# A decoder layer with a mixture of experts: the routing of two batches stepped beside the experts' items, its count products and statistics pinned in trace order

## The chip, the core and the metric

The kernel runs on one core of one Trainium2 chip. The core has five engines, each with a queue of its own: TensorE (PE in the profile; its weight loads are PEld), VectorE (DVE), ScalarE (ACT), GpSimd (POOL), and SyncE (SP), which here only starts transfers. An engine runs its queue in order; semaphores let one engine wait for another. The metric is the time of one execution on the device in microseconds (us), as the median of several runs. A profile comes from one execution, which has a time and a span of its own.

## What is computed

Four batches of 512 tokens of 256 elements pass through three layers. Each is added to its input and normalised. The first is a selective state space layer, the second a gated attention over a context, the third a mixture of eight experts of which each token takes two:

```python
x = _layernorm(x + _L0_attn_ref(x, ...))
x = _layernorm(x + _L0_xattn_ref(x, ctx_1024, ctx_1024, ...))
x = _layernorm(x + _L0_ffn_ref(x, gate_w, w1, w2, w3))

def _L0_ffn_ref(hidden_states, gate_w, w1, w2, w3):
    ...
    logits = x @ gate_w
    mult, sel = _sparse_mixer_routing(logits)      # the two best experts and their weights
    w = jnp.sum(mult[:, :, None] * (sel[:, :, None] == jnp.arange(E)[None, None, :]), axis=1)
    h = jax.nn.silu(jnp.einsum('th,ehf->etf', x, w1)) * jnp.einsum('th,ehf->etf', x, w3)
    out = jnp.einsum('etf,efh,te->th', h, w2, w)
```

The change touches the end of the second layer and the beginning of the third.

## The kernel before

**Who sets the order.** The kernel is written on a library that plans it: the code is traced once, and a planner then fills each engine's queue. By its own estimates of durations it takes, whenever an engine is free, the instruction whose inputs are ready, and of several the one traced first. So the trace order is a priority, not the order on the chip, and the queues are fixed before the kernel runs. `tc.keep_in_program_order(ins)` forbids the planner one thing: to put `ins` ahead of the instruction traced just before it on the same engine. It adds no wait on the chip. Only what is later in the trace can still overtake a pinned instruction, if that one isn't ready.

**Attention** (`attend_fast`). Work goes by pairs (batch b, pair of heads p), eight in all. The loop over n = 0 to 8 (L1178) has four turns each, `tb`. A turn traces the scores of pair n (`pq`, L1026, then `ct` on ScalarE, L1037, and the triangle on GpSimd, L1038), the values of pair n-1 (`ph`, L1046), and in the first turn the gather of pair n-2 (`gather`, L1051): `ph` is copied to `hT`, turned by products into `pth` (L1060), and `hraw` (L1064) takes it from there. PSUM for `pth` comes from a pool of two banks, `pt`, which later also holds the experts' transposes.

**The tail of a batch.** After the second pair of a batch is gathered, `finish(b)` (L1084) becomes a generator in the list `tails`. `step()` (L1166) runs one piece of the first tail; the loop calls it twice per turn (L1199, L1200). Counting pieces from 0, they are, before:

- 0: scales `den`, `vr` (with a square root on ScalarE). 1: the logits `base` (L1110 to L1120), then the first choice (`route`, L1683). 2: the second choice. 3: `hv` (L1127) on VectorE and the sum with x1 on GpSimd (L1134).
- 4 (`close`, L1800): `hot` (L1713), the mark of the chosen experts, then `norm_stats` (L59): four times `bn_stats` (L64) and `bn_aggr` (L65) on VectorE, a square root on ScalarE (L67), a reciprocal.
- 5: the count products, five of them (L1717), and `rstd`. 6: the normalised rows `x` on ScalarE (L1815) and their writes to `xds` and `yd` by SP (L1820).
- 7: positions of tokens, from `posm` (L1727) to `hi` (L1739). 8: `olo` (L1745), eight times `oval` (L1750) and a position product (L1754). 9 and 10: `by` (L1765) and the tables of tokens, weights and destinations (`tables`, L1644). 11: the weights of the two experts (L1776 to L1789, with Exp). 12: a transpose of them (L1792), and their writes to `wds` by SP (L1798).

Batch b's tail is appended in turn 0 of n = 2b + 3, so batch 2's pieces 0 to 7 are traced at n = 7 and 8 to 12 at n = 8; batch 3's tail is appended after the loop and is traced as a whole between two calls of `work` (L1934).

**The experts.** `work` (L1339) takes items in a line. An item fetches its token rows with an indirect transfer on GpSimd (`fetch`, L1244; two items ahead), transposes them (L1277, copied to `xgT`, L1281), and runs `up` (L1284): chunks of 16 (one block of 128 tokens) or 8 products (two blocks) into `pu` (L1292), Silu on ScalarE (L1297), `ht` on VectorE (L1298), with a yield after each chunk. `pu` has three banks. (The trace shows two instructions for each f32 product; products are counted here as it shows them.) Then `down` of the item before runs (L1316), scaled (L1336) by weights fetched in `weigh` (L1306), and is added to `yd` (L1322).

The **early** items (experts 0 and 1, one block each, four chunks each) need only the tables of batches 0 and 1. The **middle** items (experts 3 to 7, two blocks, eight chunks) need the tables and rows of batch 2, the **late** ones those of batch 3. All of the rest of the kernel is TensorE's work on these items.

Of the kernel before, what the change touches and what calls it, by code (L numbers as in the profile page):

```python
# [2 lines left out]

# [40 lines left out]
def decoder_kernel(ctx: ExitStack, tc: tile.TileContext, t: dict, out: bass.AP):  # L44
    nc = tc.nc
# [10 lines left out]
        nc.sync.dma_start(out=c, in_=src)  # L56
        return c

    def norm_stats(sp, src, n, tag):  # L59

        st = sp.tile([P, n, 6], F32, tag=tag + "st", name=tag + "st")
        mv = sp.tile([P, n, 2], F32, tag=tag + "mv", name=tag + "mv")
        for i in range(n):
            nc.vector.bn_stats(out=st[:, i, :], in_=src[:, i, :])  # L64
            nc.vector.bn_aggr(out=mv[:, i, :], in_=st[:, i, :])  # L65
        sd = sp.tile([P, n], F32, tag=tag + "sd", name=tag + "sd")
        nc.scalar.activation(sd, mv[:, :, 1], AF.Sqrt, bias=eps5)  # L67
# [934 lines left out]
    def attend_fast(ap, hrp, np_, pt, tri, onw, mix, part, gatew, close, rt, route):  # L1002
# [4 lines left out]
        with ExitStack() as hs:  # L1007
# [170 lines left out]
            for n in range(len(pairs) + 1):  # L1178
                nxt = []
                if n and pairs[n - 1][1] == 0:  # L1180
                    hraw = hrp.tile([P, NB, NH, DH + 1 + NE], F32, tag="hraw", name="hraw")
                    sq2 = hrp.tile([P, NB, NH], F32, tag="sq2", name="sq2")
                if n:
                    po = ph.tile([P, S], F32, tag="ph", name="ph")
                for tb in range(NB):
                    if n == B:
                        for _ in late:
                            pass
                    elif n:
                        next(late, None)  # L1190
                    if n < len(pairs) and tb < NB - 1:
                        nxt += scores(*pairs[n], (tb,) if tb < NB - 2 else (tb, tb + 1))
                    if tb == 0 and sums is not None:
                        gathered(*sums)
                    if tb == 1 and n in (1, 1 + NH):
                        residual(n // NH)
                    if n:
                        values(*pairs[n - 1], tb, cts[tb], po)
                    step()  # L1199
                    step()  # L1200
                if n:
                    sums = (*pairs[n - 1], po, hraw, sq2)
                cts = nxt
# [11 lines left out]
    def experts(o, fast):  # L1215
# [120 lines left out]
                nc.scalar.activation(y[:, g, :], ps[:, g, :], AF.Copy, scale=wg[:, g : g + 1])  # L1336
                scatter(yd, v, c, y[:, g, :], compute_op=ALU.add)

        def work(visits, weights, ahead=(), between=None, pending=None):  # L1339

            after = [e for e, _ in (*visits, *ahead)][len(weights) :]
            line = [(n, v, cols) for n, (_, its) in enumerate(visits) for v, cols in its]
            xgs = [fetch(v, cols) for _, v, cols in line[:2]]
            for i, (n, v, cols) in enumerate(line):
                G = len(cols)
                xT_ = turn(xgs.pop(0), G)
                w1, w3, w2 = weights[n]
                ht = inner(G)  # L1350
                for _ in up(xT_, G, w1, w3, ht):
                    pass
                if i + 2 < len(line):
                    xgs.append(fetch(*line[i + 2][1:]))
                if pending is not None:
                    down(*pending)
                pending = (v, cols, ht, w2)
                if (i == 0 or line[i - 1][0] != n) and after and len(weights) < n + 3:
                    weights.append(weights_of(after.pop(0)))
                if between is not None:  # L1360
                    between(i)
            return weights[len(visits) :], pending
# [189 lines left out]
    def layers23(fast):  # L1552
# [4 lines left out]
        with ExitStack() as rest:  # L1557
# [125 lines left out]
            def route(b, base):  # L1683
# [30 lines left out]
                yield  # L1714
                pc = bank[:, 32 : 32 + 5 * NE].rearrange("p (n e) -> p n e", e=NE)
                for i in range(5):
                    nc.tensor.matmul(  # L1717
                        pc, one_b if i else tri_b, hot[:, 4 - i : 9 - i, :],
                        start=(i == 0), stop=(i == 4),
                    )  # L1720
                yield
                NK = 2 * NB
# [26 lines left out]
                for j in range(NK):  # L1749
# [1 line left out]
                        oval[:, j, :], i128, hi[:, j : j + 1],  # L1751
                        vv[:, b * NK + j : b * NK + j + 1], ALU.is_equal, ALU.mult,
                    )
                    nc.tensor.matmul(  # L1754
                        pk, olo[:, j, :], oval[:, j, :], start=(j == 0), stop=(j == NK - 1)
                    )
                nc.vector.tensor_tensor(count, pc[:, NB], count, ALU.add)
                if 1 <= b < B - 1:
# [30 lines left out]
                nc.vector.reciprocal(wk, su)  # L1789
                yield  # L1790

                nc.tensor.transpose(bank[:NK, 384:], wk, ident)  # L1792
                wkT = rt("wkT", [NK, P])
                nc.scalar.copy(wkT, bank[:NK, 384:])
                for v in range(max(b - 1, 0), 3):
# [4 lines left out]
            def close(b, hv, routing=None):  # L1800
# [2 lines left out]
                if routing is None:  # L1803
                    routing = route(b, logits(b, hv))
                next(routing)
                mv, rs = norm_stats(np_, hv, NB, "n2")
                yield
                next(routing)
                rstd[b] = rt("rstd", [P, NB])
                nc.vector.tensor_copy(rstd[b], rs)  # L1810
                ms = np_.tile([P, NB], F32, tag="n2ms", name="n2ms")
# [111 lines left out]
            o.htp, o.sip, o.yp, o.xtp, o.np3, o.fin, o.pup, o.pop, o.x1 = (  # L1923
                htp, sip, yp, xtp, np3, fin, pup, pop, x1
            )
            if tails:
                *done, last = tails
                for tail in done:
                    for _ in tail:
                        pass  # L1930
            else:
                last = iter(())
            weights, pending = xp.work(xp.early, weights, xp.mid)
            for _ in last:  # L1934
                pass
            weights, pending = xp.work(
                xp.mid + xp.late, weights, [xp.final], lambda i: overflow() if i == 1 else None,
                pending,
            )
            return xp.finale(xp.final, weights[0], pending)  # L1940

# [118 lines left out]
```

## Time and profile before

| | |
|---|---|
| median of 3 runs | 681.87 us (680.82 to 684.33) |
| the profiled execution | 681.57 us |
| its span, first to last instruction | 679.7 us |
| granted TensorE clock, mean of the span | 0.978 |
| TensorE busy | 645.8 us (95%) |
| stage from 200 to 292 us: TensorE busy, granted clock | 77.68 of 92 us, 0.89 |
| in the same stage: VectorE, ScalarE, GpSimd busy | 75.02, 52.95, 52.66 us |
| from 292 to 640 us: TensorE busy, granted clock | 348.00 of 348 us, 1.00 |

The granted clock is the share of full speed that the chip's throttle allowed TensorE. A line of the timeline gives the start, the duration, the engine, the line of the kernel and the operation, what it writes and reads, how many are merged, and in brackets the engine's idle time before it and what ended that. A line of the waits names who waited for whom, the total, how often, and the longest. A busy engine isn't one at full speed, and an engine that is idle costs nothing where it isn't the bound.

Four points of the timeline are used below: attention's last values end at 253.78 us, expert 0's first product starts at 262.86, its transposed token rows at 261.68, and the first middle item's first product at 290.50. A batch's GpSimd sums (L1134) take 0.73 us each, four to a batch.

### The profile page before, as it was taken

To read this page: it belongs to the slowest core of one execution; us is meant where nothing else is said; L and a number is where in the kernel's file an instruction comes from. 1 tells how busy PE (TensorE), PEld (TensorE's weight loads), DVE (VectorE), ACT (ScalarE), POOL (GpSimd) and SP (SyncE) were. 2 spreads that over 40 slices of the span, in tenths; PEclk is the share of its full clock that TensorE was granted. 3 is DMA by queue.
4 is the path that set the end of the run, shared out by engine and by line. 5 is a ranking of instruction groups with operands and counts; after the bars stand their busy time and mean duration, and the time that the engine had idled before them with its cause. 6 is when DMAs were issued, how large, how long until landed. Compare 5 with 4: busy or idle time off the path is not lost. (4 is left out here: it accounts for less than half of the span.)

```text
span 679.7 us, 9237 instructions
## 1 busy us (share of the span) xinstructions
PE 645.8 (95%) x3447; PEld 497.9 (73%) x3447; DVE 307.8 (45%) x799; ACT 241.1 (35%) x473; POOL 209.0 (31%) x244
## 2 busy tenths in 40 slices
PE   6999999999997987899999999999999999999994
PEld 2434577766353447788888888888888899999993
DVE  1969658797557899662222221111211121121641
ACT  3965472132775754541121221112111111111452
POOL 0033400000564572743423244322432323423202
PEclk9999999999997996999999999999999999999998
DMA  8300501004603066856755335644463524883531
GB/s 279 121 1 0 186 1 32 31 1 160 242 1 124 9 196 216 285 170 209 220 169 179 86 94 154 194 153 137 150 209 78 152 78 148 272 316 86 176 113 36
DMA packets 61671, 92.89 MB, mean 137 GB/s; under 512 B 8904, under 2 KB 48784, under 8 KB 61360
## 3 DMA queue, kind: packets, MB, share of 16 engines
q1 hardware_dynamic: 52432, 80.51, 34.7%
q0 software_dynamic: 8096, 9.60, 7.2%
q10 hardware_dynamic: 1088, 2.10, 0.9%
q8 instruction: 29, 0.48, 0.3%
q14 instruction: 26, 0.21, 0.1%
HBM read 78.78 MB, written 14.06 MB: 137 GB/s over the span
## 5 line engine op out<-in xcount | busy, mean ns | idle before, releaser
L1292 PE MATMUL pu<-xgT,w 128*128 128x128 f32 (+1 forms) x1600 | 266.3, 327 | 1.0 <-DVE ht L1298 0.9
L1292 PEld LDWEIGHTS pu<-xgT,w 128*128 128x128 f32 x1600 | 243.0, 193 | 22.7 <-ACT x L1391 1.1
L1298 DVE TENSOR_TENSOR ht<-pu,si 128x256 f32<-128x256 f32 x148 | 62.6, 424 | 229.5 <-ACT si L1297 229.2
L1316 PE MATMUL po<-w,ht 128*128 128x256 f32 x592 | 136.7, 381 | 0.0
L1297 ACT ACTIVATE si<-pu 128x256 f32<-128x256 f32 x148 | 56.8, 384 | 195.6 <-PE pu L1292 195.3
L1316 PEld LDWEIGHTS po<-w,ht 128*128 128x128 f32 x592 | 109.8, 191 | 14.6 <-ACT y L1336 0.6
L1322 POOL DMA_INDIRECT yd<-y,tab x33 | 53.3, 1614 | 143.3 <-ACT y L1336 125.7
L232 PE MATMUL xz<-xT,win 128*128 128x512 f32 x128 | 58.3, 616 | 6.3 <-DMA xT<-in_xT 5.8
L1248 POOL DMA_INDIRECT xg<-xd,tab x37 | 36.8, 993 | 82.7 <-PE pt L1277 59.5
L232 PEld LDWEIGHTS xz<-xT,win 128*128 128x128 f32 x128 | 24.9, 198 | 38.8 <-issue 30.4
L1336 ACT ACTIVATE y<-po,wg 128x256 f32<-128x256 f32 x33 | 15.6, 474 | 93.8 <-PE po L1316 93.8
L1038 POOL TENSOR_TENSOR ct<-ct,tri 128x128 f32<-128x128 f32 x64 | 32.7, 530 | 34.0 <-ACT ct L1037 33.4
L460 PE MATMUL fpy<-mt,xs 128*128 128x384 f32 (+3 forms) x128 | 36.8, 438 | 0.5 <-DVE fsz L464 0.5
L255 DVE SCALAR_TENSOR_TENSOR acc<-xp,convw,acc 128x1024 f32<-128x1024 f32 x24 | 29.3, 1286 | 14.2 <-ACT acc L250 14.2
L1037 ACT ACTIVATE ct<-pq,eT 128x512 f32<-128x512 f32 (+3 forms) x64 | 29.9, 524 | 15.3 <-PE pq L1026 15.2
L1307 POOL DMA_INDIRECT wg<-wd,tab x33 | 31.9, 967 | 9.9 <-issue 9.6
L1026 PE MATMUL pq<-x1T,ctxT 64*128 64x512 f32 (+3 forms) x128 | 33.0, 486 | 1.6 <-ACT ct L1037 1.2
L1281 DVE COPY xgT<-pt 128x512 f32<-128x512 f32 (+1 forms) x22 | 12.5, 569 | 41.4 <-PE pt L1277 41.4
L460 PEld LDWEIGHTS fpy<-mt,xs 128*128 128x128 f32 x128 | 22.1, 190 | 12.3 <-issue 6.2
L485 PE MATMUL fpo<-fwout,fsz 128*128 128x256 f32 x128 | 28.9, 382 | 0.1
L485 PEld LDWEIGHTS fpo<-fwout,fsz 128*128 128x128 f32 x128 | 23.8, 190 | 4.7 <-issue 0.8
L1026 PEld LDWEIGHTS pq<-x1T,ctxT 64*128 64x128 f32 x128 | 13.7, 188 | 17.5 <-issue 8.0
(260 smaller groups left out, 612.9 us busy)
## 6 DMA issues: line engine op xcount, KB each, us to landing
w<-in_w SPq DMA_DIRECT2D x57, 1024.0 KB
xd<-x SPq DMA_DIRECT2D x9, 512.0 KB
xT<-in_xT ACTq DMA_DIRECT2D x4, 512.0 KB
ctxT<-in_ctxT SPq DMA_DIRECT2D x1, 2048.0 KB
val<-in_ctx SPq DMA_DIRECT2D x4, 512.0 KB
fxr<-in_x SPq DMA_DIRECT2D x4, 512.0 KB
yd<-x SPq DMA_DIRECT2D x4, 512.0 KB
x<-yd SPq DMA_DIRECT2D x4, 512.0 KB
```

The costliest lines, as they stand in the source:

```text
L232: nc.tensor.matmul(ps, win[:, k, c * P : (c + 1) * P], xT[:, k, b * S : (b + 1) * S], start=(k == 0), stop=(k == 1),)
L460: nc.tensor.matmul(ps[:, j * P :], xs[j][:, c, :], mt[b][j], start=(j == 0), stop=(j == NB - 1),)
L485: nc.tensor.matmul(ps, sz[:, c, b * S + i * P : b * S + (i + 1) * P], wout[:, c, :], start=(c == 0), stop=(c == NC - 1),)
L1026: nc.tensor.matmul(pss[e][:, cols[-1]], ctxT[rows, p, s0 : s0 + P], x1T[rows, p, s0 : (b + 1) * S], start=True, stop=True,)
L1038: nc.gpsimd.tensor_tensor(ct[:, :P], ct[:, :P], tri, ALU.mult)
L1248: nc.gpsimd.indirect_dma_start(out=xg[:, g, :], out_offset=None, in_=xds[min(v, 2)][:, :], in_offset=bass.IndirectOffsetOnAxis(ap=tok[v][: ...
L1292: nc.tensor.matmul(ps[:, j, u, :], w[:, k, (f + u) * P : (f + u + 1) * P], xT_[:, k, :N], start=(k == 0), stop=(k == 1),)
L1297: nc.scalar.activation(si, ps[:, 0].rearrange("p u n -> p (u n)"), AF.Silu)
L1298: nc.vector.tensor_tensor(ht[:, f * N : (f + U) * N], ps[:, 1].rearrange("p u n -> p (u n)"), si, ALU.mult)
L1307: issue = nc.gpsimd.indirect_dma_start(out=wg, out_offset=None, in_=wds[min(v, 2)][:, :], in_offset=bass.IndirectOffsetOnAxis(ap=wat[v][:, ...
L1316: nc.tensor.matmul(ps, ht[:, (f * G + g) * P : (f * G + g + 1) * P], w2[:, f, :], start=(f == 0), stop=(f == NF - 1),)
L1322: return nc.gpsimd.indirect_dma_start(out=rows[:, :], out_offset=bass.IndirectOffsetOnAxis(ap=dest[v][:, c : c + 1], axis=0), in_=src, in_ ...
```

## The change

1. In the loop of `attend_fast`, `step()` isn't called any more at n = 7 and n = 8. The tail of batch 2, which is appended at n = 7, therefore leaves the loop untouched; `tails` then holds the tails of batches 2 and 3.
2. `work` takes an iterator `beside` and advances it once after each chunk of `up`. Before the early items the tail of batch 2 is given to it, and before the middle items that of batch 3, both through `zip_longest` with itself, that is two pieces per chunk. What is left of batch 2's tail after the early items is traced then.
3. In `close`, the piece with `rstd` no longer runs the count products. They come after the normalised rows, as a piece of their own: three pieces behind `hot` in place of one. A tail has 14 pieces now, 0 to 13: the count products are 7, positions 8, position products 9, tables 10 and 11, weights 12, their transpose 13.
4. `bn_stats` of this norm, the count products, the position products and the transpose of the weights are pinned with `keep_in_program_order`.

Piece by chunk, then: batch 2's pieces 0 to 7 follow the four chunks of expert 0, two by two, and 8 to 13 the first three of expert 1; batch 3's follow the first seven of the first middle item's eight chunks. Batches 0 and 1 stay in the loop, with one piece more each.

```diff
-    def norm_stats(sp, src, n, tag):
+    def norm_stats(sp, src, n, tag, keep=False):
...
-            nc.vector.bn_stats(out=st[:, i, :], in_=src[:, i, :])
+            bn = nc.vector.bn_stats(out=st[:, i, :], in_=src[:, i, :])
+            if keep:
+                tc.keep_in_program_order(bn)
             nc.vector.bn_aggr(out=mv[:, i, :], in_=st[:, i, :])
...
-                    step()
-                    step()
+                    if n < len(pairs) - 1:
+                        step()
+                        step()
...
-        def work(visits, weights, ahead=(), between=None, pending=None):
+        def work(visits, weights, ahead=(), between=None, pending=None, beside=iter(())):
...
                 for _ in up(xT_, G, w1, w3, ht):
-                    pass
+                    next(beside, None)
...
                 for i in range(5):
-                    nc.tensor.matmul(
-                        pc, one_b if i else tri_b, hot[:, 4 - i : 9 - i, :],
-                        start=(i == 0), stop=(i == 4),
+                    tc.keep_in_program_order(
+                        nc.tensor.matmul(
+                            pc, one_b if i else tri_b, hot[:, 4 - i : 9 - i, :],
+                            start=(i == 0), stop=(i == 4),
+                        )
                     )
...
-                    nc.tensor.matmul(
-                        pk, olo[:, j, :], oval[:, j, :], start=(j == 0), stop=(j == NK - 1)
+                    tc.keep_in_program_order(
+                        nc.tensor.matmul(
+                            pk, olo[:, j, :], oval[:, j, :], start=(j == 0), stop=(j == NK - 1)
+                        )
                     )
...
-                nc.tensor.transpose(bank[:NK, 384:], wk, ident)
+                tc.keep_in_program_order(nc.tensor.transpose(bank[:NK, 384:], wk, ident))
...
                 next(routing)
-                mv, rs = norm_stats(np_, hv, NB, "n2")
+                mv, rs = norm_stats(np_, hv, NB, "n2", True)
                 yield
-                next(routing)
                 rstd[b] = rt("rstd", [P, NB])
...
-            if tails:
-                *done, last = tails
-                for tail in done:
-                    for _ in tail:
-                        pass
-            else:
-                last = iter(())
-            weights, pending = xp.work(xp.early, weights, xp.mid)
-            for _ in last:
+
+            *done, last = tails or [iter(())]
+            third = chain(*done)
+            third = zip_longest(third, third)
+            weights, pending = xp.work(xp.early, weights, xp.mid, beside=third)
+            for _ in third:
                 pass
             weights, pending = xp.work(
                 xp.mid + xp.late, weights, [xp.final], lambda i: overflow() if i == 1 else None,
-                pending,
+                pending, zip_longest(last, last),
             )
```

More of the change, by code (lines that the diff above doesn't have):

```diff
@@ L1 @@
 from contextlib import ExitStack
+from itertools import chain, zip_longest
 from types import SimpleNamespace
```

## The prediction, made before the changed kernel was run

> **What bounds the kernel now.** I read the busy shares first, then the slices, then the waits of TensorE, then its timeline where the slices show a hole. Columns of the first fence: busy microseconds with the share of the span, and the span in 40 slices of 17 us, in tenths.
>
> ```profile
> PE 645.8 (95%) x3447; PEld 497.9 (73%) x3447; DVE 307.8 (45%) x799; ACT 241.1 (35%) x473; POOL 209.0 (31%) x244
> ...
> PE   6999999999997987899999999999999999999994
> ...
> DVE  1969658797557899662222221111211121121641
> ...
> PEclk9999999999997996999999999999999999999998
> ```
>
> TensorE is the bound: 9 in nearly every slice, and all of the time from 292 to 640 us (the windows view gives 348.00 of 348.00 us busy there). The exceptions lie in slices 12 to 16 (204 to 289 us), where PE falls to 7 and 8, PEclk to 7 and 6, and DVE stands at 7 to 9: the stage in which attention and routing overlap and the experts begin. Time won there comes off the end, as the experts run behind it without a gap. The waits of TensorE between 200 and 292 us (total, times, longest):
>
> ```profile
> PE prt L1717 <- DVE hot L1713: 7.8, 4, 3.1
> PE pth L1060 <- DVE thr L1700: 3.6, 1, 3.6
> PE pq L1026 <- ACT ct L1037: 1.2, 1, 1.2
> ```
>
> The first line is the count products, once per batch: TensorE runs its queue in order and stood still four times until VectorE had the choice (`hot`). Its timeline across batches 2 and 3 (start, duration, what, idle before):
>
> ```profile
> 257.43 2.29 PE L1060 MATMUL pth<-mix,hT 128*128 128x146 f32 x8 [3.65 <-DVE thr L1700]
> 260.65 0.19 PE L1717 MATMUL prt<-hot,tri_b 128*128 128x40 bf16 x1 [0.94 <-DVE hot L1713]
> ...
> 262.86 3.78 PE L1292 MATMUL pu<-xgT,w 128*128 128x128 f32 x16
> ...
> 287.75 0.19 PE L1717 MATMUL prt<-hot,tri_b 128*128 128x40 bf16 x1 [3.10 <-DVE hot L1713]
> ...
> 290.50 0.71 PE L1292 MATMUL pu<-xgT,w 128*128 128x256 f32 x2
> ```
>
> Three holes, then 290.50, where the first middle item begins. And why `hot` was late, on VectorE and ScalarE:
>
> ```profile
> 282.85 0.43 DVE L64 BATCH_NORM_STATS2 n2st<-hv 128x6 f32<-128x256 f32 x1 [4.20 <-POOL hv L1134]
> 283.20 0.17 DVE L1700 TENSOR_REDUCE thr<-base 128x4 f32<-128x32 f32 x1
> ...
> 286.30 0.30 ACT L67 ACTIVATE n2sd<-n2mv,eps 128x4 f32<-128x4 f32 x1 [4.68 <-DVE n2mv L65]
> ```
>
> `base` was ready at 278.66, but the first statistic stood ahead of the choice and waited 4.20 us for GpSimd's sum. The planner had put it there to fill gaps; the chip's GpSimd was later.
>
> **The change, part by part.** The sum is made against the profiled execution, 681.57 us (span 679.7 and 1.9 around it); the median shown is 681.87, 0.3 higher, so nothing is converted.
>
> *Statistics behind the choice (all batches).* Nothing is added or removed: 4 x 0.42 + 4 x 0.16 = 2.3 us of VectorE per batch move behind `hot`. The choice is 12 instructions of about 0.17 us, 2.1 us alone; it took 204.37 to 211.09 in batch 0 (6.7 us). Without the statistics between, and with GpSimd still slowing some of it, I take 4. Batch 0's products waited 2.49 us and batch 1's 1.24; I count 2.0 and 0.5 back. What is late next is ScalarE: it is 1.8 to 2.0 us busy in each 2 us from 208 to 214, and the normalised rows now leave about 2 us later; nothing on the path reads them before the expert fetches. So no more than **2.5 us** for batches 0 and 1 together, though 1.18 us of waiting for `ct` and a dip of the clock (210 to 214 at 0.50) would be there to win too.
>
> *Routing of batch 2 beside the early items.* Before, its pieces were traced in the last two turns of the attention loop, ahead of the last two gathers and of expert 0; now they come behind. The 3.65 us hole is this: the last gather's products needed the bank that `hraw` (L1064) frees; that copy's input was there at 252.34, and it ran at 256.83, behind choice and statistics. With the copy at about 254.5, the gather starts near 254.7: 1.2 us of the hole stay (`hT` is there at 254.53). Gather 1.3, the next two copies 1.0, transposes 0.7, `xgT` 0.4 give expert 0's first product near 258.3 instead of 262.86.
>
> *Products pinned and moved back.* For batch 2 the count products may not run before expert 0's fourth chunk, the eight position products (L1754) not before expert 1's first, the transpose not before its third. The planner cannot pull them forward into a wait.
>
> What bounds the start of the middle items now? Two candidates.
> (a) TensorE's work. From 253.78 to 290.50 it was idle 8.0 us (3.65, 0.94, 3.10 and small ones). The slow clock cost 3.5 us near 258 to 266 (8 gathers 2.29 for 1.26, 4 transposes 1.09 for 0.60, 16 products 3.78 for 16 x 0.114) and 1.4 near 288 (4 transposes 1.10 for 0.60, 4 down products 1.92 for 1.03). 290.5 - 12.9 = 277.6, or 278.8 with the 1.2 that stay.
> (b) The token table of the middle items, which is now later in the order. Expert 0's 64 products of 0.114 end at 258.3 + 7.3 = 265.6; then counts; from `posm` to the last `oval` took 5.1 us in batch 1 (235.92 to 240.99), with two `ht` (0.42 each) between 5.9; to the table 1.3: 273.2. Then two row fetches, 1.25 apart, and 3.8 to landing (the median of these fetches): 278.3; transposes and copy 1.3: 279.6. The old table stood at 270.2, 17 us before use: this move spends cover, not time. If it is gone, each microsecond of the table is one of the end.
>
> I take 280.8, with 1.2 for VectorE being slower than its instructions alone: 290.5 - 280.8 = **9.7 us**. The 20 us up to there hold some 3 us of VectorE's own `ht`, ahead of the routing now.
>
> *Routing of batch 3 beside the first middle item.* The same instructions, behind chunk 0 to 6. The 3.10 us hole is already in (a). New waits: the pinned products in the middle item stand ahead of that item's later chunks. Below: 0, if VectorE is done. Above: 5.0 us, `posm` to the last `oval` in batch 3. Nearest row: the position products lost 2.4 us to `oval` in five waits over four batches. I take **1.7 us** for batches 2 and 3. SP's queue gets the row and weight writes in the same place; GpSimd's sums lie behind the first fetches as before (the 4.20 us wait stays with the statistics, now behind the choice, with three `pu` buffers of 1.75 us to cover it). Tables for the late items have five items of some 20 us each before use.
>
> *One more piece per batch, fewer steps in the loop:* no instruction, nothing.
>
> Sum: 681.6 - 2.5 - 9.7 + 1.7 = **671.1 us**.
>
> **Two rules weighed.** *The clock.* The rows: 2.49 us idle, with 1.18 shortly before, was followed by 0.50 granted at 210 to 214; 3.65 by 0.50 at 258 to 264; 3.10 by 0.50 at 288; 1.24 by nothing. "TensorE: Matmul & The Clock Gate" (Part 1) of the Trainium skill says that a window of about 3.4 us of idleness halves the clock. By the rule only the 3.65 hole cost clock, and (a) would be 1.4 us less; by the rows shorter holes do too. I take the rows; since (b) sets the start, the sum stays.
> *A rule against the change.* "ScalarE: Activation LUTs" (What ACT_TABLE_LOAD costs) puts each change of table set at 2.66 us, load and drain, and batch 2's Exp now falls between expert 0's Silu: one Exp and one Silu load more. The row is 1.283 us, with the activation 0.01 to 0.02 after it (260.53, then 261.82). By the rule 5.3 us of ScalarE, above the 3.6 us that two spare `pu` buffers of 1.8 cover: 1.7 us on TensorE. By the row 2.6, covered: nothing. The row decides.
>
> **Rivals.**
> 1. *The table comes late.* VectorE has `ht` ahead of the routing and some 25 us of work between 253 and 278, so the table may slip to 279. For: it is 1.8 to 2.0 busy in most 2 us windows there. Against: it also idled 4.20. Then the middle items begin at 286.5, 4 us won: 681.6 - 2.5 - 4 + 1.7 = **676.8**.
> 2. *The order hardly changes.* The planner already let pieces lag about a turn behind their trace, and a pin only forbids earlier. Then only statistics help: 681.6 - 2.5 = 679.1, and with half of that **680.3**. Against: batch 2 and 3 do fall behind other work.
> 3. *Slower: position products block TensorE.* Each of the eight waits for its `oval` with expert products behind it in the queue. If the planner counts VectorE too fast, TensorE stands the 5 us from `posm` to the last `oval`, twice, and runs at half clock for as long as after the old holes (3 us lost): 16 instead of 1.7, so 681.6 - 2.5 - 9.7 + 16 = **685.4**. For: all four count products waited this way. Against: `oval` waits were short. It decides from 12 us of such waits on.
>
> **How the numbers follow.** Forecast 0.60, rivals 0.12, 0.11 and 0.17. No change means within 0.5%, 678.5 to 685.3, about what a measurement of this kernel can tell. Faster: forecast less its tail and most of rival 1, 0.67. Same: rival 2 and pieces of its neighbours, 0.16. Slower: most of rival 3 and its longer stands, 0.17. Range: below, no slip, no new waits and the clock of batch 0 (1.2, 1.7, 2.4, and 1.5 of the `ct` waits) give 664; above, rival 3 at 686.
>
> **What would show it.** Right: no idle at L1717; the hole before the last gather near 1 us; granted clock 1.00 from 253 to 292; the first 256-column product of the experts near 278 with batches 0 and 1 counted in; L64 behind L1713. Wrong: that product still near 288, a wait at L1277 for a fetch, or waits at L1754 of several microseconds.

## The result: half a per cent slower, and the profile after

The changed kernel took 685.77 us in the median (683.8 to 687.4, 19 runs), the kernel before 682.84 beside it (679.57 to 685.29, 19 runs): a ratio of 1.0048, 95% interval 1.0032 to 1.0063. The forecast was 671.1 us, faster than before; the kernel came out slower.

The same changed kernel, run again, took 676.0 and 677.0 us on two chips and 684.9, 686.0 and 686.4 us on three others, so whether the change gains or loses differs here from chip to chip. Each chip was measured in one session only, so chip and session can't be told apart: "chip" below stands for both.

First the page of the changed kernel: busy time of each engine, and three rows of the span in 40 slices.

```profile
PE 643.7 (94%) x3447; PEld 494.8 (72%) x3447; DVE 307.7 (45%) x799; ACT 244.6 (36%) x476; POOL 208.5 (31%) x244
...
PE   6999999999997899859999999999999999999994
...
DVE  1969568796658889534212111121111111111642
...
PEclk9999999999998999979999999999999999999997
```

Counted from 0, slices 14 and 15 (238 to 272 us) have risen from 8 and 7 to 9, the clock of slice 15 from 6 to 9. Slice 17 (290 to 307 us) has fallen from 9 to 5 and its clock from 9 to 7. TensorE's waits, in total, times and longest, name it:

```profile
PE pu L1296 <- DVE ht L1302: 8.9, 2, 8.0
PE prt L1722 <- DVE hot L1717: 6.6, 2, 4.2
...
PE pt L1281 <- DMA xg<-xd,tab: 2.2, 1, 2.2
PE prt L1800 <- DVE sc L1707: 1.1, 1, 1.1
```

The second line stood at 7.8 us in four waits before; it is 6.6 in two. The first is new: one wait of 8.0 us for `ht`. In the timeline (start, duration, what, idle before):

```profile
254.11 1.47 PE L1063 MATMUL pth<-mix,hT 128*128 128x146 f32 x8
...
257.24 4.96 PE L1296 MATMUL pu<-xgT,w 128*128 128x128 f32 x42
...
264.49 0.18 PE L1722 MATMUL prt<-hot,tri_b 128*128 128x40 bf16 x1
...
281.31 0.80 PE L1281 MATMUL pt<-ident,xg 128*128 128x128 f32 x4 [2.17 <-DMA xg<-xd,tab]
...
290.13 0.26 PE L1722 MATMUL prt<-hot,one_b 128*128 128x40 bf16 x4
...
295.63 0.95 POOL L1311 DMA_INDIRECT wgf<-wd,tab  x1 [0.31 <-issue]
298.85 0.19 DVE L1733 TENSOR_TENSOR posm<-prt,count 128x32 f32<-128x32 f32 x1 [9.06 <-remote]
...
301.06 1.08 DVE L1302 TENSOR_TENSOR ht<-pu,si 128x256 f32<-128x256 f32 x3
...
301.53 2.08 PE L1296 MATMUL pu<-xgT,w 128*128 128x256 f32 x4 [8.04 <-DVE ht L1302]
```

Down to 281.31 this is what was forecast: the second half of the last gather without its hole (3.65 us before), expert 0 at 257.24 instead of 262.86, batch 2's counts without a wait, and the experts' first 256-column product at 282.94 instead of 290.50. Then the new part. Batch 3's count products end at 290.39, yet `posm`, which needs nothing else that is late, starts at 298.85. It stands ahead of three `ht` in VectorE's queue, the `ht` free the `pu` banks, and so TensorE idles 8.04 us, and the granted clock is 0.50 from 297 to 307.

Where the time went can be told from three marks in each trace: the copy into `xgT` of the first middle item, that of the second, and the end. From the second copy to the end every profile of an unshortened kernel in this study takes 369.6 to 371.6 us.

| profile | first copy | second copy | between | second copy to end | span |
|---|---|---|---|---|---|
| before | 289.04 | 309.56 | 20.5 | 370.1 | 679.7 |
| changed | 282.14 | 313.35 | 31.2 | 369.7 | 683.0 |

So -6.9 us up to the first copy, +10.7 in the first middle item, -0.4 behind: +3.3. Both the gain and the loss are in the stage the change touches.

### The profile page after: what moved, and what is told of

The parts are those of the page before. It is cut to its first block, busy times and chain, and to the rows that moved or that the text cites. A ratio compares the mean times of both kernels' runs of the same rounds, so it can differ in the third digit from the quotient of the medians.

```text
span 683.0 us, 9244 instructions
## 1 busy us (share of the span) xinstructions
PE 643.7 (94%) x3447; PEld 494.8 (72%) x3447; DVE 307.7 (45%) x799; ACT 244.6 (36%) x476; POOL 208.5 (31%) x244
## 5 line engine op out<-in xcount | busy, mean ns | idle before, releaser
L1029 PE MATMUL pq<-x1T,ctxT 64*128 64x256 f32 (+3 forms) x128 | 31.7, 500 | 0.4 <-DVE lh L1113 0.3
L488 PEld LDWEIGHTS fpo<-fwout,fsz 128*128 128x128 f32 x128 | 23.8, 190 | 4.7 <-issue 0.8
L1049 PE MATMUL ph<-ct,val 128*64 128x512 f32 (+3 forms) x128 | 25.3, 469 | 0.8 <-POOL ct L1041 0.8
```

Of the source, the lines that this page charges most:

```text
L488: nc.tensor.matmul(ps, sz[:, c, b * S + i * P : b * S + (i + 1) * P], wout[:, c, :], start=(c == 0), stop=(c == NC - 1),)
L1029: nc.tensor.matmul(pss[e][:, cols[-1]], ctxT[rows, p, s0 : s0 + P], x1T[rows, p, s0 : (b + 1) * S], start=True, stop=True,)
```

## The experiments

**The changed kernel again, and the kernel before, on several chips.** `after_again`, `after_third`, `after_fourth`, `after_fifth`, `after_sixth` are the changed kernel, `before_own` and `before_own2` the one before; no line differs.

> The changed kernel once more, unaltered, for a second profile. Its first profile has a hole of 8.04 us on TensorE inside the first middle item (293.5 to 301.5 us), where the signals of finished chunks reach ScalarE up to 8.5 us late. Theory A (the hole belongs to the kernel): it stands at the same place again, 6 to 10 us long, and the time is 0.3 to 0.6% above before. Theory B (the hole is an accident of that one execution): it is not there, and the profiled time is 675 to 679 us; then the loss of 2.9 us in the median is somewhere else.

> The changed kernel once more, unaltered, beside the variants below. Its two profiles so far differ by one hole alone: 8.04 us of TensorE in front of L1296 at 301.53 and half clock behind it, together 11.8 us. Theory A, the hole comes or stays away from one execution of the same program to the next: the times fall in two groups some 10 us apart, one at 673 to 680 us and one at 683 to 688. Theory B, the hole belongs to the chip or the session: all executions here lie in one of the two groups. If the hole is absent in the profile, TensorE's waits read 6.6 (L1722), 2.2 (L1281), 1.1 (L1800) again and no wait for ht above 1 us.

> The changed kernel, unaltered, as the measure for the next two on this chip. In all profiles so far the end lies 369.6 to 370.3 us behind the second middle item's copy into xgT. Theory A: two sorts of chips; with some 6,026 records of semaphore changes the stretch from the first to the second middle item's copy takes 20.2 us and the time is 675 to 679 us; with some 5,275 it takes 30 us and the time is 684 to 688. Theory B: the two do not go together (for instance 5,275 records and 20 us).

> The kernel before, unaltered, for a profile of it from the same chip as the next three. On the chip where the changed kernel was at 686.4 us, every profile held about 750 fewer records of semaphore changes (5,268 to 5,318) than where it was at 677.0 (6,019 to 6,030). Theory A, that is the chip's, and the disturbance strikes only where many signals fall together: if the next run shows the hole, this profile has some 5,270 records too, yet its stretch from the copy into xgT of the first middle item to that of the second stays at 20 to 21 us, and the time at 680 to 683. Theory B, the lost records are the changed kernel's own: some 6,018 here.

> The changed kernel, unaltered: the mark of which sort of chip this is. Theory: records of semaphore changes, the stretch from the first middle item's copy to the second's and the time go together: about 6,026 records, 20 to 22 us and 673 to 680 us, or about 5,275, 30 us and 684 to 688. If another pair comes (5,275 records and 20 us), the two are not bound together.

> The changed kernel, unaltered: 684 to 688 us with about 5,275 records of semaphore changes and 30 to 31 us from copy to copy, or 673 to 680 us with about 6,026 and 20 to 22 us, as in five measurements so far.

> The kernel before, unaltered, for a profile beside the next two. If its records of semaphore changes number some 5,275 (a chip where the changed kernel has the hole): theory A, here too they fall from 140 to 190 per 10 us to some 40 between 280 and 310 us, but the stretch from the first middle item's copy to the second's, 20.5 us elsewhere, grows by no more than 2 us, since the median of this kernel is only 0.5 to 1 us higher on such chips; theory B, they do not fall at all, and only the changed kernel's order brings it about. If there are some 6,018 records: 20.5 us again.

Measured, with the number of records of semaphore changes in the whole trace (a change is how an engine or a transfer tells another that it is done) and those between 280 and 310 us; the copies are in us, and the ratio is to the kernel before on the same chip:

| kernel | chip | median us | ratio, 95% | records | in 280-310 | first copy | between copies |
|---|---|---|---|---|---|---|---|
| changed, `after_again` | a | 677.02 | 0.9937 (0.9908-0.9967) | 6026 | 477 | 281.4 | 20.2 |
| changed, `after_fourth` | b | 676.01 | 0.9922 (0.9898-0.9947) | 6026 | 515 | 284.1 | 21.7 |
| changed, the result's | - | 685.77 | 1.0048 (1.0032-1.0063) | 5276 | 122 | 282.1 | 31.2 |
| changed, `after_third` | c | 686.37 | 1.0062 (1.0039-1.0085) | 5274 | 135 | 282.8 | 30.1 |
| changed, `after_fifth` | d | 686.01 | 1.0046 (1.0031-1.0061) | 5290 | 122 | 281.5 | 30.9 |
| changed, `after_sixth` | e | 684.89 | 1.0015 (0.9991-1.0039) | 5242 | 129 | 285.2 | 29.8 |
| before, `before_own` | b | 681.29 | 1.0001 (0.9985-1.0018) | 6016 | 484 | 288.6 | 20.5 |
| before, `before_own2` | e | 682.71 | 0.9998 (0.9979-1.0016) | 5296 | 323 | 290.2 | 20.0 |

The marks go together in all six profiles of the changed kernel: many records, 20 to 22 us from copy to copy, a gain; few records, 30 to 31 us, a loss (on chip e one that isn't clear of noise). The few records are the chip's, not the change's, since the kernel before has 5,296 too on chip e; but there its item still takes 20.0 us, and between 280 and 310 us it loses fewer records (323, where the theory had some 120). The times of one kernel on one chip did not fall into two groups, as one theory had it. What the hole is not: another order, for the queues are the same program. The timeline of `after_fourth`, where it is absent:

```profile
293.36 0.25 PE L1722 MATMUL prt<-hot,one_b 128*128 128x40 bf16 x4
...
293.65 0.19 DVE L1733 TENSOR_TENSOR posm<-prt,count 128x32 f32<-128x32 f32 x1 [2.67 <-PE prt L1722]
...
295.86 1.08 DVE L1302 TENSOR_TENSOR ht<-pu,si 128x256 f32<-128x256 f32 x3
...
296.57 1.03 PE L1296 MATMUL pu<-xgT,w 128*128 128x256 f32 x4
```

Here `posm` starts 0.04 us after the last count product; in the result's profile it was 8.46 us. The records of the traces show how the signals come: TensorE's changes are 1.7 us apart in `after_again` (284.15 to 289.33 us, one for each chunk), but stand at 288.87, 293.84 and 298.76 us in the result's trace, some 4.9 us apart.

**The statistics.** `only_stats` is the kernel before with this alone (and `norm_stats` as in the change):

```diff
-                mv, rs = norm_stats(np_, hv, NB, "n2")
+                mv, rs = norm_stats(np_, hv, NB, "n2", True)
```

> The kernel before with one part of the change alone: bn_stats of this norm pinned behind hot. Theory A (the pin costs by itself in batches 0 and 1, where hot came no earlier): 1 to 3 us slower than before. Theory of the prediction: 2.5 us faster or more, since the wait of 4.20 us of batch 3's statistics no longer stands ahead of the choice.

`no_stats` is the changed kernel with `"n2"` in place of `"n2", True`; `pin_late` has `"n2", b > 1`, so that the pin holds for batches 2 and 3 only.

> The changed kernel without the pin of bn_stats. If the pin is what costs: 2 to 4 us faster than the changed kernel, that is no slower than before. If the loss is the first middle item's hole alone: within 1.5 us of the changed kernel.

> The changed kernel with the statistics held behind the choice only in the last two batches (b > 1). Theory: the pin lengthens the waits for the choice in batches 0 and 1 (4.24 and 2.39 us with it, 2.42 and 1.23 without it, the other pins making no difference), and helps only batch 3, where without it VectorE stands 4.81 us for GpSimd's sum with the choice and the fetch's copy behind it. Then the waits at L1722 are about 2.4 and 1.2 again, every later event is 2 to 3 us earlier, and the kernel is 2 to 3 us faster than the changed one. Rival: the pin's later waits are repaid where the batch's next stage waits anyway (the last gather of heads), so nothing is gained: within 0.7 us of the changed kernel.

Measured: `only_stats` 683.62 us, ratio 1.0022 (1.0002 to 1.0043), chip a; `no_stats` 682.40, 1.0022 (1.0003 to 1.0042), chip a, 5.4 us above the changed kernel there; `pin_late` 683.00, 1.0007 (0.9982 to 1.0032), chip c, 3.4 below the changed kernel there. The two waits for the choice in batches 0 and 1 follow the pin and nothing else: 2.49 and 1.24 us without any pin, 2.42 and 1.23 in `no_stats` (1.24 in `pin_late`), 4.24 and 2.38 in `only_stats`. The pin does bring batch 0's choice forward: from the ready `base` to `hot` it takes 6.8 us in the changed kernel and in `only_stats`, 7.6 before. But the planner's queue has the count products earlier by more. Before, products of scores and values stood ahead of them (206.08 to 208.66 us), which now stand behind, and TensorE reaches them at 205.97. In the timelines of the kernel before (two lines) and the changed one:

```profile
210.92 0.17 DVE L1713 TENSOR_TENSOR hot<-oh 128x32 bf16<-128x32 f32 x1
...
211.15 0.19 PE L1717 MATMUL prt<-hot,tri_b 128*128 128x40 bf16 x1 [2.49 <-DVE hot L1713]
...
209.97 0.19 DVE L1717 TENSOR_TENSOR hot<-oh 128x32 bf16<-128x32 f32 x1
...
210.21 0.19 PE L1722 MATMUL prt<-hot,tri_b 128*128 128x40 bf16 x1 [4.24 <-DVE hot L1717]
```

Batch 3 looked like the place where the pin is worth its price. VectorE in `no_stats`:

```profile
284.76 0.43 DVE L65 BATCH_NORM_STATS2 n2st<-hv 128x6 f32<-128x256 f32 x1 [4.81 <-POOL hv L1137]
...
288.15 0.68 DVE L1285 COPY xgT<-pt 128x512 f32<-128x512 f32 x1
```

The statistic stands in VectorE's queue for GpSimd's sum, and behind it now the middle item's own copy into `xgT`, at 288.15 instead of 281.4 on the same chip. But `pin_late` has this pin in batches 2 and 3 and its copy is at 288.1 all the same. Its TensorE:

```profile
256.45 1.97 PE L1063 MATMUL pth<-mix,hT 128*128 128x146 f32 x8 [2.41 <-ACT hT L1058]
...
261.53 10.05 PE L1296 MATMUL pu<-xgT,w 128*128 128x128 f32 x64 [1.13 <-DVE xgT L1285]
```

A hole in front of the last gather is back (2.41 us), and expert 0's 64 products take 10.05 us at a lower clock. So the two pins in batches 0 and 1, bad for their own waits, leave an order behind them that brings the first copy forward by 5.3 us on chip c (288.1 to 282.8); what the pin in batch 3 is worth beside them was not tried. My theory on `pin_late` held for the two waits, but not for what follows: later events were not 2 to 3 us earlier. On chip a the first copy stands at 294.0 us with the pin alone, at 288.1 with all but the pin, and at 281.4 with both: neither part has the gain by itself.

**Which move, which pins.** `last_between` traces batch 3's tail ahead of the middle items; `batch3_only` traces batch 2's in one piece ahead of the early ones; `no_pe_pins` drops `keep_in_program_order` from the three kinds of products. From the changed kernel:

```diff
 # last_between
+            for _ in last:
+                pass
             weights, pending = xp.work(
                 xp.mid + xp.late, weights, [xp.final], lambda i: overflow() if i == 1 else None,
-                pending, zip_longest(last, last),
+                pending,
             )
 # batch3_only
-            third = chain(*done)
-            third = zip_longest(third, third)
-            weights, pending = xp.work(xp.early, weights, xp.mid, beside=third)
-            for _ in third:
+            for _ in chain(*done):
                 pass
+            weights, pending = xp.work(xp.early, weights, xp.mid)
```

> The changed kernel, but batch 3's tail is traced between the early and the middle items as before, no longer beside the first middle item; all pins stay. Theory A (the hole is made by batch 3's pieces beside the item): the hole goes, the first middle item starts near 283 and the next near 305, and the time is 6 to 10 us below the changed kernel, 675 to 680. Rival (only the place of the hole changes): 684 to 688.

> The changed kernel with batch 2's tail traced as a whole ahead of the early items, as before; only batch 3's tail steps beside the first middle item. With the run that has batch 3's tail between the items (676.2 against 677.0 for the changed kernel), it tells which of the two moves carries the gain. Theory: batch 2's move alone does (it brings expert 0's products forward by 5.6 us and fills the hole in front of the last gather), so here the last gather's wait of about 3.6 us is back, expert 0's first product stands near 262.5, and the time is 681 to 683 us. Rival: batch 3's tail beside the middle item carries it, since the 3.10 us wait at the counts and the half clock behind it are gone: 675 to 678 us.

> The changed kernel without the three pins on TensorE (counts L1722, positions L1761, weights' transpose L1800); the statistics stay pinned and the two tails stay beside the items. Theory: the tracing order of the pieces already puts these products behind the items' ones, the order of TensorE's queue hardly changes, and the time is the changed kernel's within 1 us. Rival: without the pins the planner draws position products forward, in front of chunks of the item, where they wait for oval: one to three waits of 0.5 to 3.6 us at L1761, as in the kernel before with only the statistics pinned (3.63 us), and 2 to 5 us more than the changed kernel.

`last_between`, chip a: 676.22 us, 0.9909 (0.988 to 0.9939), not to be told from the changed kernel there; that chip has no hole, so the run says nothing of what makes it. `batch3_only`, chip c: 680.75, 0.9966 (0.9947 to 0.9986). `no_pe_pins`, chip c: 680.09, 0.9969 (0.9948 to 0.9991). The theory on `batch3_only` missed: expert 0 begins at 259.6 (257.6 in `after_third`, 262.9 before), and the first copy is at 283.9 (282.8 and 289.0), most of the gain. But this run isn't batch 2's old place, as its expectation has it: `step()` still isn't called at n = 7 and 8, so the tail stays out of the attention loop and behind the last gathers, and only the stepping beside the early items is undone. That stepping is worth some 1 to 2 us up to the item. No run keeps batch 2's tail in the loop with the rest of the change, so what leaving the loop is worth alone stays open. Both theories on `no_pe_pins` missed as well: without the pins on TensorE the first copy is at 284.0, and the kernel is faster on this chip, not equal or slower. On chip c both beat the changed kernel by about 6 us, with 25.6 us from copy to copy instead of 30.1.

**What makes the signals late.** `last_between2` and `last_between3` are `last_between` again; `spread` and `spread2` give a chunk one piece of batch 3's tail in place of two:

```diff
-                pending, zip_longest(last, last),
+                pending, last,
```

> The changed kernel with batch 3's tail traced between the early and the middle items, so that only batch 2's tail steps beside items; the three pins on TensorE and the one on the statistics stay. Theory: the hole needs batch 3's tail in the first middle item (there posm waits in VectorE's queue for a late signal of TensorE, with three ht behind it), so this version takes 20 to 22 us from copy to copy on every chip, and is 676 to 678 us here too, faster than both kernels even where the changed one stands at 686. Rival: the late signals come from the load of that stretch whatever is traced there; then, where the changed kernel is at 686, this one is above 683 too.

> The changed kernel with one piece of batch 3's tail to a chunk of the middle items in place of two, so that the tail spans the first middle item and most of the second. Theory: the hole is a matter of how densely TensorE's, VectorE's and the queues' signals fall in the first item; with half of them per item the hole is shorter, the copy-to-copy stretch 20 to 24 us, and the time 675 to 680 us on a chip where the changed kernel is at 686 (where that one is at 677: within 2 us of it). Rival: it is the one wait of posm in front of the ht; then the hole only moves, the stretch stays near 30 us on such a chip, and the time within 2 us of the changed kernel on either.

> The changed kernel with batch 3's tail ahead of the middle items. Where after_fifth is at 673 to 680: within 2 us of it, as twice before (676.2 against 677.0, 677.4 against 676.0). Where after_fifth is at 684 to 688: theory A, the hole needs the tail inside the item: 675 to 679 us and 20 to 22 us from copy to copy; theory B, the place alone makes signals late: above 682 us, with a wait of several us in or before that item.

> The changed kernel with one piece of batch 3's tail to a chunk. Where after_fifth is at 673 to 680: within 2 us of it, as before (677.4 against 676.0; its first item takes 18.3 us from copy to copy, the second takes the rest). Where after_fifth is at 684 to 688: theory A, half the tail's signals per item shorten the hole: 20 to 24 us from copy to copy and 676 to 680 us; theory B, they do not: within 2 us of after_fifth.

On chip b (many records) `last_between2` took 677.41 us, 0.9951 (0.9932 to 0.997), and `spread` 677.35, 0.9954 (0.9938 to 0.997): the changed kernel's time within 2 us. On chip d (few) `last_between3` took 688.13, 1.0077 (1.0052 to 1.0102), and `spread2` 681.73, 0.9988 (0.9969 to 1.0008), against 686.01. `spread2` takes 23.8 us from copy to copy, as its theory A had it, but its time is above the 676 to 680 us of theory A and below those of theory B. Its signals are late in the same stretch (TensorE's changes stand 4.9 to 5.0 us apart there too); yet no `posm` stands ahead of the `ht` there, and TensorE loses 2.37 and 1.65 us to `ht` instead of 8.04. My theory that the hole needs batch 3's tail inside the item fell. TensorE's waits of `last_between3`:

```profile
PE prt L1800 <- DVE wk L1797: 9.6, 2, 9.4
```

The hole only has another name; it comes in the same stretch of time wherever the tail is traced. What is common to that stretch showed in GpSimd's timeline. In the changed kernel it issues 16 indirect transfers without a break: six row fetches, a gather of weights, a scatter, two more fetches, six more gathers of weights, about one each 1.25 us, from 276.07 to 296.6 us. The last of the late signals arrive when that train ends. From the start of its last issue to the release of the stalled VectorE instruction it was:

| profile | last issue | VectorE goes on | difference |
|---|---|---|---|
| changed, the result's | 295.63 | 298.85 | 3.22 |
| `after_third` | 295.95 | 299.18 | 3.23 |
| `after_fifth` | 294.69 | 298.00 | 3.31 |
| `after_sixth` | 297.98 | 301.47 | 3.49 |
| `last_between3` | 294.99 | 298.21 | 3.22 |

The difference is about what such a gather takes from its issue to its landing, 3.3 us in the median in the trace of before; whether the signals wait for that landing is not shown. In the kernel before, the longest run is of nine (270.42 to 282.07 us); GpSimd's own sums and waits break up the rest. The train alone doesn't make the lateness: on chips a and b the changed kernel has the same 16 issues, and nothing is late. `no_weigh` cuts the train: it leaves out the gathers of the rows' weights of early and middle visits, seven of them in that train, and scales by one.

```diff
         def weigh(wg, v, c):
+            if v < 2:
+                nc.gpsimd.memset(wg, 1.0)
+                return
```

> The changed kernel without the gathers of the rows' weights of the early and middle items (each product is scaled by one instead), so six gathers fewer stand between 284 and 296 us, and later ones are gone too; its end is not to be compared, only the stretch from the first to the second middle item's copy. On a chip with the hole: theory A, the lateness comes from the number of DMA signals in the stretch: it falls from 30 us to under 25. Theory B, it is TensorE's and VectorE's own signals, or the mere volume of data (the gathers of weights carry 128 numbers each): still 28 us or more. On a chip without it: 20 to 22 us as in the changed kernel.

On chip e, beside `after_sixth`: 21.2 us from copy to copy, not 29.8. (Its end is not compared, as stated: its last part takes 374.2 us; the median is 681.83.) In its timeline the line numbers are three higher:

```profile
289.81 0.16 POOL L1312 MEMSET wg<- 128x1 f32 x2
...
293.33 0.26 PE L1725 MATMUL prt<-hot,one_b 128*128 128x40 bf16 x4
...
293.62 0.19 DVE L1736 TENSOR_TENSOR posm<-prt,count 128x32 f32<-128x32 f32 x1 [2.67 <-PE prt L1725]
```

GpSimd's last fetch of the stretch was issued at 288.87, and at 293.62 `posm` follows its product at once. The records between 280 and 310 us rise from 129 to 274. Shown, then, by one profile on one chip with few records: the lateness goes with those gathers. It isn't that transfers are slower there: between 276 and 300 us the median packet of 1,024 bytes takes 46 to 47 ns in all 20 traces, and one of four bytes 9 ns. Open: whether the gathers' number, their small pieces (16 packets of 32 bytes and 16 of four bytes each) or the unbroken run counts; and whether the lateness is in the signals themselves or comes of recording them, as every time here has a profile's span beside it. A version that keeps all gathers but issues them later was not tried.

## Why the prediction was wrong, step by step

- *Bound, and where time can be won.* Right: everything is decided before the second middle item; behind it the time is constant within 2 us.
- *Statistics, -2.5.* Wrong in sign. The step looked for what is late next only in the normalised rows ("nothing on the path reads them before the expert fetches") and counted 2.0 and 0.5 us back; the waits grew from 2.49 to 4.24 and from 1.24 to 2.39 us. Two things were wrong. The choice was taken at 4 us without the statistics between; it took 6.9 (203.22 to 210.16), no less than before (6.7), since other work took their place and some of its instructions ran 0.34 to 1.19 us where 0.17 stood. And I took the consumer's place in TensorE's queue as fixed, while the planner moved the consumer forward too. What the pins of batches 0 and 1 do serve, an order in which the first middle item's copy comes 5.3 us earlier than in `pin_late`, I had not seen.
- *Expert 0 near 258.3.* Right: 257.24 (256.3 to 259.6 in six profiles of the changed kernel), and no wait at batch 2's counts. The reason is supported in part: `batch3_only`, with the tail out of the loop but not stepped, gets to 259.6, and `pin_late` shows that the pin is needed too.
- *First middle item, (b), 280.8 less the statistics' share, 278.3.* It began at 282.94: 4.6 late. 2.5 of this is the credit for the statistics that did not come. The rest is the table, "to the table 1.3": its last row was ready at 276.54, not 273.2. The `oval` ended at 270.25, 4.9 us after `posm` (5.9 in the sum), but then VectorE took 6.3 us to the last row, with batch 3's `hv` (1.22), three `ht` and instructions that took 0.6 to 0.8 us in place of 0.2 to 0.3 between. The 1.3 was too low for the rows of before as well: in batch 1 this stretch took 4.1 us (240.99 to 245.04). A wait for the fetch of 2.17 us came in front of the transposes; this is a piece of rival 1, which let the table slip to 279.
- *Batch 3 beside the first middle item, "I take 1.7", 5.0 above.* This is the step that failed, for the measured result. Product to second copy grew from 19.06 to 30.41 us: 11.35 where 1.7 stood, hence 9.65 of the 13.7 us by which the profile (684.82) misses the forecast. The rest is mostly the late start of the item above. The step priced waits of position products on `oval` alone, and in the profile TensorE's products waited for none; the wait was VectorE's, for a signal of TensorE that came 8.46 us late on chips of one sort, with three `ht` behind it that free the `pu` banks. The sum had no term for a late signal, nor for what stands behind `posm` in VectorE's queue. Its nearest row was misread too: of the 2.4 us in five waits, 2.1 are of weight loads (PEld), and the products themselves lost 0.3. The trace of before came with 6,018 records and showed no such lateness, so its size could not be read there; and GpSimd's 16 issues in one run, which the change brings onto the item, are in no term of the sum.
- On chips with many records the step was near: 20.2 and 21.7 us from copy to copy against 20.5. There the direction holds, with 676.0 and 677.0 us, 5 to 6 above the forecast: the statistics and the table.
- *Rival 3* gave 685.4, close to the measured number, by another cause, so by luck: it had position products blocking TensorE with batch 2 and 3 alike.
- *The clock, rows against rule.* The 4.24 us wait was followed by 0.50 from 210 to 214, as either would have it. But waits before the same product differ: behind 2.24 us in front of L1281 the clock stayed at 1.00 in `after_again` (first two lines below), and behind the shorter 1.83 it fell to 0.50 in `after_fourth` (284 to 287 us). The length of the wait, on which my rows and my reading of the rule both went, doesn't tell these apart. It was worth 1.7 us: the four `po` products behind took 1.82 instead of 1.03, and the 32 of the item 8.01 instead of 7.14.

```profile
280.54 0.81 PE L1281 MATMUL pt<-ident,xg 128*128 128x128 f32 x4 [2.24 <-DMA xg<-xd,tab]
281.18 1.03 PE L1320 MATMUL po<-w,ht 128*128 128x256 f32 x4
...
283.24 0.80 PE L1281 MATMUL pt<-ident,xg 128*128 128x128 f32 x4 [1.83 <-DMA xg<-xd,tab]
283.88 1.82 PE L1320 MATMUL po<-w,ht 128*128 128x256 f32 x4
```

  What does tell them apart is where the idle time falls. In every trace here the granted clock changes only at steps of 3.41 us (its stretches between 208 and 291 us before the change are 6.83, 40.96, 10.24, 20.48 and 3.41 us), and TensorE's busy share of one step goes with the clock of the next: 0.55 from 279.0 to 282.4 us in `after_again`, 0.46 from 280.6 to 284.0 in `after_fourth`: the 1.83 us fell wholly into one step, the 2.24 us were split over two. From 215 to 310 us, over all 20 traces, the clock fell after each of the 33 full-speed steps that were busy 0.475 or less, and after none that was busy 0.478 or more. (The ends of products are modelled, and between 200 and 215 us, in attention, the clock also fell behind 0.61 to 0.65 in three traces, so this share holds for that stretch only.)
- *The table load:* the row held; every load between 257 and 283 us took 1.28 us. There are three more than before (32 against 29), where two were counted; no wait of TensorE came of it.

## What to carry to other kernels

A pin on a producer can move its consumer too when a planner fills the queues: price the wait anew from where the consumer will stand, and expect parts of such a change not to add (the statistics' pin alone cost 2.3 us, and taking it out of the whole cost 5.4). When a step is moved, look at which long run of transfers it is moved beside, and do not put in front of an engine's queue an instruction that waits for a distant signal while others free the buffers of the bound engine. Measure a gain of one per cent on several chips before keeping it: of the versions tried, one piece to a chunk (`spread`) was the more even, 0.9954 and 0.9988 of the kernel before on the two sorts, though the second is not told from no change.

## What the hardware did that I had not expected

Two sorts of chips showed up among six measurements, by a mark that no timing view shows: some 6,020 or some 5,280 records of semaphore changes for the same work. Nearly all that is missing are changes made by transfers that land (3,841 to 3,850 records in nine traces, 3,115 to 3,218 in eleven); the engines' own are 2,167 to 2,180 and 2,094 to 2,138. On the second sort, between 280 and 310 us, 122 to 135 changes were recorded where the first sort had 477 to 515, and in the changed kernel signals of TensorE reached VectorE up to 8.5 us late, until 3.2 to 3.5 us after the last of 16 indirect transfers was issued. The kernel before is hardly touched there (682.71 against 681.29 us), though not because nothing is late: its timeline on chip e shows ScalarE waiting in the early items, where time was to spare before the old 3.10 us hole, which is 0.67 here. That wait ends at 281.30 us while GpSimd's run of nine is still being issued, so not every late signal holds out to the end of a run.

```profile
281.30 0.38 ACT L1297 ACTIVATE si<-pu 128x256 f32<-128x256 f32 x1 [3.33 <-remote]
...
288.92 0.18 PE L1717 MATMUL prt<-hot,tri_b 128*128 128x40 bf16 x1 [0.67 <-DVE hot L1713]
```
